# Depthwise convolution of a ConvNeXt block: filter matrices by 16 channels in three buffers, x read image by image

## The chip, the cores and the metric

The kernel runs on one core of one Trainium2 chip. The metric is the device time of one execution in microseconds; lower is better. All data are float32.

## The reference, cut to what matters

The input x is 32 images of 384 channels of 28 x 28 pixels. Layer 0 is a ConvNeXt block, layer 1 a channel gate:

```python
y = conv_general_dilated(x, dw_w, padding=[(3, 3), (3, 3)], feature_group_count=384)  # 7x7, one filter a channel
y = layernorm over channels (y + dw_b) * ln_g + ln_b
y = gelu(y @ w1 + b1)                       # 384 -> 1536
y = grn_g * (y * nx) + grn_b + y            # nx from the norm of y over the pixels
x = x + y @ w2 + b2                         # 1536 -> 384
logits = (means, maxima and minima of x over pixels, through small matrices)
x = sigmoid(logits + x)
```

The change lies in the first line, the depthwise convolution.

## The kernel before

**Two stretches.** First the depthwise convolution of all 32 images, whose result goes to HBM (`yd`, `yl`). Then, image by image, the feed-forward part: normalise, the up-projection (`up`, L901), GELU and its response norm, the down-projection (`down`, L1023), the gate. Both projections are written as a fast matrix product with fewer multiplications. Its sums of weights are made during the convolution by GpSimd (`form_w`, L585 and L587) and stored to HBM (`u1d`, `u2d`).

**The convolution as matmuls.** A 28 x 28 image is cut into blocks of 7 rows and half the width (14 columns, with the border 18). For one channel, such a block is a vector of KP = 126 numbers (18 columns by 7 rows), and the 7 x 7 filter is a banded matrix of 126 x 126 entries and more. The kernel doesn't build it entry by entry: `sequences` (L400) writes each channel's filter once as a row of FL = 268 numbers to HBM (`fs`), and `load_t` (L416) reads this row 126 times, each time shifted, into the 126 partitions of a tile `tmat`. It takes three transfers: 112 partitions of inner columns and two of 7 partitions for the edge columns, whose filters are cut. One `load_t` covers TC = 8 channels; 8 x 268 numbers are 8,576 bytes in a partition. There are NK = 48 such groups, and four `tmat` buffers.

**The x side.** `load_x` (L459) brings 16 channels of NB = 8 images into 128 partitions, one channel of one image (784 numbers, 3,136 bytes) in each, in an order of channel first and image second. There are eight buffers (seven in `room`, and `xi_last`). `pad_x` (L482) copies it with borders into `xpad`, TensorE turns it (`turn_x`, L516) into PSUM, and VectorE writes it to `xt` (L530, and L532 for the rows at the image's end). A block of XC = 16 channels (`k`) takes four such loads for the 32 images, and 24 blocks take 96.

**The order.** It is written out by hand: the loop over s (L736) takes 8 channels a turn. `conv` (L642, matmuls at L653) works on two channels at a time, four times a turn; ScalarE and VectorE move its results to `yc` (L669, L661); between these `spread` (L696) pads and turns x of the next block of 16. `load_t(s + 3)` is issued at the start of turn s. Every second turn `store` (L677) writes 16 channels to HBM. All transfers of the convolution but the filters' rows go through SP's queue in the program's order, and SP waits for a transfer's buffer before it issues the next one.

Of the kernel before, what the change touches and what calls it, by code (L numbers as in the profile page):

```python
# [8 lines left out]
F32 = mybir.dt.float32  # L9
# [4 lines left out]
P = 128  # L14
C = 384
# [4 lines left out]
NT = HW * HW  # L20
# [14 lines left out]
KP = RW * KW  # L35
NV = HW // RW
NJ = 2 * NV
NI = NV + 1
XC = 16
TC = 8  # L40
YC = 16
NB = P // XC
# [8 lines left out]
FL = 2 * PR * RW + 2  # L51
# [150 lines left out]
def convnext_gate_kernel(  # L202
# [13 lines left out]
    nc = tc.nc  # L216
    B = x.shape[0]
# [7 lines left out]
    fs = [dram.tile([3, P + 1, FL], F32, name=f"fs_{cb}") for cb in range(CB)]  # L225
# [131 lines left out]
    with ExitStack() as one:  # L357
        tp = one.enter_context(tc.tile_pool(name="tp", bufs=1))
# [33 lines left out]
        grp_a = scratch([CB, R])  # L392


        NT2 = 4
        tmat = [tp.tile([P, TC, FL], F32, name=f"tmat_{i}") for i in range(NT2)]
        nc.vector.memset(tab[:, 0], 0.0)
        nc.gpsimd.memset(tab[:, 1:], 0.0)

# [13 lines left out]
        nc.vector.memset(zrow, 0.0)  # L413
        NK = C // TC

        def load_t(s, parts=1):  # L416
            base = fs[s * TC // P]
            n = TC // parts
            for i in range(parts):
                t = tmat[s % NT2][:, i * n : (i + 1) * n, :].rearrange("k c m -> k (c m)")  # L420
                start = base.offset + (s * TC % P + i * n) * FL
                for v, e0, ne in ((0, 1, KW - 2), (1, 0, 1), (2, KW - 1, 1)):
                    nc.sync.dma_start(
                        t[e0 * RW : (e0 + ne) * RW],
                        bass.AP(
                            tensor=base.tensor,
                            offset=start + v * (P + 1) * FL + e0,
                            ap=[[1, ne], [PR, RW], [1, n * FL]],
                        ),
                    )  # L430
# [3 lines left out]
        NPAD = 3  # L434
        NWARM = 9
        xpad = [tp.tile([P, 2, NV, KW, RW], F32, name=f"xpad_{i}") for i in range(NPAD)]
# [15 lines left out]
        NX = C // XC  # L452
# [6 lines left out]
        def load_x(i):  # L459

            k, g = divmod(i, NG)
            n = i % NXI
            t = xis[i] = xi_last if n == NXI - 1 else room[:, n * NT : (n + 1) * NT]
            base = x[g * NB, k * XC : k * XC + 1, :]
            nc.sync.dma_start(
                t,
                bass.AP(
                    tensor=base.tensor,
                    offset=base.offset,
                    ap=[[NT, XC], [C * NT, NB], [1, NT]],  # L470
                ),
            )

# [34 lines left out]
        def turn_x(i, h, xt, eng=nc.vector):  # L508

            g = i % NG  # L510
            xv = xt[:KP].rearrange("p c (j b) -> p j c b", b=B)[:, h * NI : (h + 1) * NI]
            xv = xv[:, :, :, g * NB : (g + 1) * NB]
            pt = psx.tile([P, 4, P], F32, tag="pt", name=f"pt_{i}_{h}")
            for j in range(NV):
                keep(
                    nc.tensor.transpose(  # L516
                        pt[:KP, j, :],
                        xpad[i % NPAD][:, h, j].rearrange("p e r -> p (e r)"),
                        ident,
                    )  # L520
                )
            src = pt[:KP].rearrange("p j (c q) -> p j c q", q=NB)
            copies = [(xv[:, 1:NV], src[:, : NV - 1], None)]
            for v, j in enumerate((NV, 0)):
                copies.append((xv[:, j], src[:, NV - 1], ends[:KP, v : v + 1]))
            for d, p, mask in copies:
                if eng is nc.scalar:
                    eng.activation(d, p, AF.Identity, scale=1.0 if mask is None else mask)
                elif mask is None:
                    eng.tensor_copy(d, p)  # L530
                else:
                    eng.tensor_scalar(d, p, mask, None, ALU.mult)  # L532
# [59 lines left out]
        def pad_next(i):  # L592
            nonlocal loaded
            if i < GT:
                pad_x(i)
                while loaded < min(GT, i + 1 + NXI):
                    load_x(loaded)
                    loaded += 1

        for i in range(NG):  # L600
            load_x(i)
        xt = new_xt(0)
        for i in range(NG):
            pad_x(i)
            if i == 0:
                load_t(0, 2)
                nc.sync.dma_start(dwb, cvec[0:1, :].broadcast_to([P, C]))
            if i == NG - 2:
                for cb in range(CB):
                    if cb:  # L610
                        keep(sequences(cb))
                    keep(nc.scalar.dma_start(fs[cb][:, P:, :].rearrange("v o m -> o v m"), zrow))
            if i == NG - 2:

                nc.gpsimd.tensor_copy(tmat[1][:, 0, :1], xpad[i % NPAD][:, 0, 0, 1, :1])
                load_t(1)
            load_x(NG + i)
            for h in range(2):
                turn_x(i, h, xt, (nc.vector, nc.scalar)[h])
# [19 lines left out]
        SK = XC // TC  # L639
        PAIRS = TC // 2  # L640

        def conv(s, c2, yc, xt):  # L642

            t = tmat[s % NT2]
            pc = psc.tile([P, 2, NJ * B], F32, tag="pc", name=f"pc_{s}_{c2}")
            for ci in range(2):
                c = 2 * c2 + ci
                for h, up_, down_ in ((0, UP_L, DOWN_L), (1, UP_R, DOWN_R)):
                    po = pc[:, ci, h * NV * B : (h + 1) * NV * B]
                    xc = xt[:KP, s % SK * TC + c, h * NI * B : (h + 1) * NI * B]  # L650
                    for n, (m0, j) in enumerate(((up_, 1), (down_, 0))):
                        keep(
                            nc.tensor.matmul(  # L653
                                po, t[:KP, c, m0 : m0 + P], xc[:, j * B : (j + NV) * B],
                                start=(n == 0), stop=(n == 1),
                            )
                        )
            cc = s * TC + 2 * c2
            cy = cc % YC
            if c2 % 2:  # L660
                nc.vector.tensor_tensor(  # L661
                    yc[:, :, :, cy : cy + 2].rearrange("p b j c -> p c j b"),
                    pc.rearrange("p c (j b) -> p c j b", j=NJ),
                    dwb[:, cc : cc + 2].unsqueeze(2).unsqueeze(3).to_broadcast([P, 2, NJ, B]),
                    ALU.add,
                )
            else:
                for ci in range(2):
                    nc.scalar.activation(  # L669
                        yc[:, :, :, cy + ci].rearrange("p b j -> p j b"),  # L670
                        pc[:, ci, :].rearrange("p (j b) -> p j b", j=NJ),
                        AF.Identity,
                        bias=dwb[:, cc + ci : cc + ci + 1],
                        scale=1.0,
                    )
# [20 lines left out]
        def spread(k, q, xn):  # L696
            for n in plan[q]:
                g, h = divmod(n, 2)
                i = k * NG + g
                if h == 0:  # L700
                    pad_next(i + 1)
                turn_x(i, h, xn)
# [32 lines left out]

        for s in range(NK):  # L736
            k, si = divmod(s, SK)
            if s + 3 < NK:
                if s == 0:
                    for i in range(2, 4):  # L740
                        nc.gpsimd.tensor_copy(tmat[i][:, 0, :1], xpad[i % NPAD][:, 0, 0, 1, :1])
                        if i == 2:
                            load_t(i)
                load_t(s + 3)
            if s in later:

                dst, src = later[s]
# [11 lines left out]
            for c2 in range(PAIRS):  # L759
                conv(s, c2, yc, xt)  # L760
                if k + 1 < NX:
                    spread(k + 1, si * PAIRS + c2, xn)
# [35 lines left out]
            i = s - U1  # L798
# [454 lines left out]
```

## Time and profile before

| what | before |
|---|---|
| median of 3 runs | 3149.55 us (3147.44 to 3153.77) |
| the profiled execution, its time | 3145.94 us |
| its span, first to last instruction | 3144.2 us |
| TensorE busy (PE) | 3048.0 us, 97% |
| VectorE (DVE), ScalarE (ACT), GpSimd (POOL) busy | 2059.3, 2146.3, 2265.0 us |
| first matmul of the up-projection | 538.5 us from the start |
| bytes moved | 653.84 MB, 208 GB/s on average |
| convolution matmuls, L653 | 3072, busy 385.9 us |

The profile is of one execution. A slice is a fortieth of the span, and its digit the busy share in tenths. Instructions stand in groups by line, engine and tile; "<-" names what ended the idle time before them. A DMA issue is an instruction of SP (SPq); the bytes then go as packets over the core's 16 DMA engines, and the DMA share is the mean busy share of the 16. A busy TensorE is not TensorE at its peak, since matmuls overlap.

### The profile page before, as it was taken

What the parts mean: (1) busy time and instruction counts of PE and PEld (TensorE: products, weight loads), DVE (VectorE), ACT (ScalarE), POOL (GpSimd) and SP (SyncE); (2) the same over time, 40 slices, a digit from 0 to 9 for tenths busy, and PEclk for the clock granted to TensorE, in tenths of its full rate; (3) what the DMA queues carried; (4) which work ended last, traced back from release to release, by engine and by line L of the source; (5) the groups of instructions that cost most, each with busy time, mean ns of one, the idle gap of its engine ahead of it and who ended that gap; (6) DMA issues with size and microseconds to landing.
All of it is one profiled execution on the core that took longest, in us unless ns stands there. A gap on an engine that the chain in (4) does not pass through costs nothing.

```text
span 3144.2 us, 48626 instructions
## 1 busy us (share of the span) xinstructions
PE 3048.0 (97%) x15913; PEld 2490.0 (79%) x15913; DVE 2059.3 (65%) x5833; ACT 2146.3 (68%) x3458; POOL 2265.0 (72%) x1776
## 2 busy tenths in 40 slices
PE   7798989999999999999999999999999999999997
PEld 7798988577777777777777777777777777777777
DVE  5565566766666666666666666666666666666665
ACT  5565664857777777777777777777777777777771
POOL 1231533398888788888888888888888888888887
PEclk9999999999999999999999999999999999999999
DMA  9999999455665666566656566555555566656545
GB/s 257 277 321 308 316 307 322 149 167 190 196 197 191 194 197 195 191 196 197 190 190 189 187 196 192 187 188 187 189 190 189 189 192 193 191 190 192 192 153 187
DMA packets 317388, 653.84 MB, mean 208 GB/s; under 512 B 30227, under 2 KB 143668, under 8 KB 308144
## 3 DMA queue, kind: packets, MB, share of 16 engines
q1 hardware_dynamic: 303520, 612.15, 62.2%
q10 hardware_dynamic: 13618, 38.58, 3.1%
q8 instruction: 130, 2.13, 0.3%
q14 instruction: 120, 0.98, 0.1%
HBM read 549.13 MB, written 101.51 MB: 207 GB/s over the span
## 4 chain that ended last, share of the span: by engine, by line
PE 76%; DMA 16%; POOL 3%; DVE 3%; issue 1%; ACT 0%; SPq 0%; ACTq 0%; POOLq 0%; DVEq 0%
PE ph_C L901 12%; PE ph_B L901 12%; PE ph_A L901 12%; DMA tmat<-fs 8%; PE pz_A L1023 7%; PE pz_C L1023 7%; PE pz_D L1023 7%; PE pz_F L1023 6%; DMA yi<-yd 3%; PE py L859 2%; PE pc L653 2%; PE pz_E L1023 2%; DMA room<-in_x 2%; PE pz_H L1023 2%; DMA yd<-yc 2%; POOL d_room L984 2%
## 5 line engine op out<-in xcount | busy, mean ns | idle before, releaser
L984 POOL TENSOR_TENSOR d_room<-y 128x588 f32<-128x588 f32 x257 | 368.4, 1439 | 348.3 <-PE pz_B L1023 199.7
L315 ACT ACTIVATE y<-y,fv,gsc 128x784 f32<-128x784 f32 x376 | 362.9, 1031 | 364.9 <-DVE gsc L937 364.9
L871 ACT ACTIVATE y<-y,fv 128x784 f32<-128x784 f32 x384 | 349.9, 945 | 195.9 <-DVE y L916 173.9
L901 PE MATMUL ph_C<-room,ws 128*128 128x392 f32 x1240 | 460.4, 493 | 2.1 <-DVE y L910 1.8
L901 PE MATMUL ph_B<-room,ws 128*128 128x392 f32 x1240 | 459.4, 493 | 2.3 <-issue 1.8
L901 PE MATMUL ph_A<-room,ws 128*128 128x392 f32 x1240 | 459.2, 492 | 2.0 <-POOL room L353 2.0
L984 POOL TENSOR_TENSOR d_room<-d_room,y 128x588 f32<-128x588 f32 x309 | 442.6, 1437 | 14.6
L653 PE MATMUL pc<-xt,tmat 126*128 126x128 f32 x3072 | 385.9, 283 | 55.1 <-DMA tmat<-fs 53.3
L653 PEld LDWEIGHTS pc<-xt,tmat 126*128 126x128 f32 x3072 | 370.2, 198 | 61.2 <-issue 49.3
L901 PEld LDWEIGHTS ph_C<-room,ws 128*128 128x128 f32 x1240 | 234.3, 190 | 178.1 <-issue 9.5
L901 PEld LDWEIGHTS ph_A<-room,ws 128*128 128x128 f32 x1240 | 235.3, 190 | 175.3 <-POOL room L353 2.6
L901 PEld LDWEIGHTS ph_B<-room,ws 128*128 128x128 f32 x1240 | 234.4, 190 | 166.9 <-DVE te L914 2.2
L984 POOL TENSOR_TENSOR d_room<-y,d_room 128x588 f32<-128x588 f32 x220 | 315.9, 1436 | 45.9 <-PE pz_A L1023 18.2
L877 ACT ACTIVATE junk<-y 128x784 f32<-128x784 f32 x384 | 328.4, 855 | 6.9
L353 POOL TENSOR_TENSOR room<-room 128x392 f32<-128x392 f32 x300 | 300.4, 1018 | 11.8
L984 POOL TENSOR_TENSOR y<-y 128x588 f32<-128x588 f32 x188 | 269.7, 1435 | 7.3
L478 ACT ACTIVATE xpad<-room 128x357 f32<-128x357 f32 (+2 forms) x320 | 188.1, 631 | 115.6 <-DMA room<-in_x 58.1
L585 POOL TENSOR_SCALAR u<-ws 128x384 f32<-128x384 f32 (+1 forms) x53 | 66.5, 1260 | 243.6 <-DMA u2d<-u 129.1
L1045 DVE TENSOR_REDUCE stq<-x 128x1 f32<-128x196 f32 x768 | 224.9, 348 | 2.5
L912 DVE TENSOR_TENSOR y<-y,ph_B 128x392 f32<-128x392 f32 x256 | 134.5, 554 | 140.1 <-ACT y L871 123.5
L910 DVE TENSOR_TENSOR y<-y,ph_C 128x392 f32<-128x392 f32 x384 | 211.3, 556 | 22.3
L1023 PE MATMUL pz_A<-d_room,u 128*128 128x196 f32 x1056 | 203.8, 329 | 0.0
(226 smaller groups left out, 6193.5 us busy)
## 6 DMA issues: line engine op xcount, KB each, us to landing
u<-u2d SPq DMA_DIRECT2D x487, 384.0 KB
ws<-u1d SPq DMA_DIRECT2D x384, 320.0 KB
ws<-u2d SPq DMA_DIRECT2D x121, 384.0 KB
yd<-yc SPq DMA_DIRECT2D x22, 2048.0 KB
tmat<-fs SPq DMA_DIRECT2D x47, 938.0 KB
yi<-yd SPq DMA_DIRECT2D x31, 1408.0 KB
x<-in_x SPq DMA_DIRECT2D x32, 1176.0 KB
out<-x ACTq DMA_DIRECT2D x31, 1176.0 KB
```

The lines of the kernel that those rows point to most:

```text
L315: eng.activation(out, in_, AF.Identity, bias=add, scale=mul)
L353: tc.keep_in_program_order(eng.tensor_tensor(d, o[in0], o[in1], op))
L478: eng.activation(dst, src, AF.Identity)
L653: nc.tensor.matmul(po, t[:KP, c, m0 : m0 + P], xc[:, j * B : (j + NV) * B], start=(n == 0), stop=(n == 1),)
L871: nc.scalar.activation(y, y, AF.Gelu, bias=b1_t[:, f : f + 1], scale=1.0)
L877: nc.scalar.activation(junk, ys[b][:, f, :], AF.Square, accum_out=ssqs[b][:, f : f + 1])
L901: nc.tensor.matmul(banks[t, bk][:, :NH], wts[t][:, i % UG, :], o[opnd], start=(first == 1), stop=True, skip_group_check=True,)
L910: nc.vector.tensor_tensor(d, d, p, ALU.add)
L912: nc.vector.tensor_tensor(d, d, p, ALU.subtract)
L984: nc.gpsimd.tensor_tensor(d[0], o[a][0], o[c][0], ALU.add if sign == "+" else ALU.subtract)
L1023: nc.tensor.matmul(pz[:, :NQ4], wt[:, i % UD, t, :], o[opnd][0][:, t, :], start=(first and t == 0), stop=(t == KD - 1), skip_group_check=True,
L1045: nc.vector.tensor_reduce(stq[:, v, m, h : h + 1], xh, AX.X, op2)
```

## The change

`load_t` now takes a block of 16 channels, the block that `xt` has, so a tile `tmat` is twice as wide and a partition gets 17,152 bytes in one run. There are three buffers in place of four, and the load is issued in every second turn, two blocks ahead. `conv` picks its 8 channels out of the 16. Independently of this, `load_x` now puts image first and channel second in the 128 partitions: 16 neighbouring channels of one image follow each other, as they do in HBM. `turn_x` reads its PSUM result in the order that belongs to it, so `xt` is the same as before.

```diff
-        NT2 = 4
-        tmat = [tp.tile([P, TC, FL], F32, name=f"tmat_{i}") for i in range(NT2)]
+        NT2 = 3
+        tmat = [tp.tile([P, XC, FL], F32, name=f"tmat_{i}") for i in range(NT2)]
...
-        def load_t(s, parts=1):
-            base = fs[s * TC // P]
-            n = TC // parts
+        def load_t(k, parts=1):
+            base = fs[k * XC // P]
+            n = XC // parts
             for i in range(parts):
-                t = tmat[s % NT2][:, i * n : (i + 1) * n, :].rearrange("k c m -> k (c m)")
-                start = base.offset + (s * TC % P + i * n) * FL
+                t = tmat[k % NT2][:, i * n : (i + 1) * n, :].rearrange("k c m -> k (c m)")
+                start = base.offset + (k * XC % P + i * n) * FL
...
-                    ap=[[NT, XC], [C * NT, NB], [1, NT]],
+                    ap=[[C * NT, NB], [NT, XC], [1, NT]],
...
-            src = pt[:KP].rearrange("p j (c q) -> p j c q", q=NB)
+            src = pt[:KP].rearrange("p j (q c) -> p j c q", q=NB)
...
-            t = tmat[s % NT2]
+            t = tmat[s // SK % NT2]
...
-                                po, t[:KP, c, m0 : m0 + P], xc[:, j * B : (j + NV) * B],
+                                po, t[:KP, s % SK * TC + c, m0 : m0 + P], xc[:, j * B : (j + NV) * B],
...
-            if s + 3 < NK:
-                if s == 0:
-                    for i in range(2, 4):
-                        nc.gpsimd.tensor_copy(tmat[i][:, 0, :1], xpad[i % NPAD][:, 0, 0, 1, :1])
-                        if i == 2:
-                            load_t(i)
-                load_t(s + 3)
+            if si == 0 and k + 2 < NX:
+                if k == 0:
+                    nc.gpsimd.tensor_copy(tmat[2][:, 0, :1], xpad[2 % NPAD][:, 0, 0, 1, :1])
+                load_t(k + 2)
```

## The prediction

> **What bounds the kernel now.** I read the page's slices first, to see which stretch differs from the rest.
>
> ```profile
> PE   7798989999999999999999999999999999999997
> DMA  9999999455665666566656566555555566656545
> ```
>
> One slice is 78.6 us. In the first seven the DMA engines are full and TensorE is not; from the eighth on it is the other way round. The change touches only code of the first stretch, the depthwise convolution. Next the busy time by stretch; the columns are length, PE, PEld, DVE, ACT, POOL, granted clock, DMA share, GB/s. The first feed-forward matmul (L901) starts at 538.5 us, so I cut at 537.
>
> ```profile
> 0.00:100.00 100.00, 74.39 (x587) 71.89 (x588) 51.42 (x127) 57.10 (x108) 15.99 (x40) 0.95 0.94 253
> 100.00:200.00 100.00, 88.45 (x753) 87.13 (x752) 57.58 (x135) 61.96 (x113) 24.00 (x20) 0.97 1.01 307
> 300.00:400.00 100.00, 93.32 (x797) 91.92 (x796) 60.91 (x141) 67.26 (x120) 51.75 (x50) 0.97 0.99 318
> 537.00:3144.00 2607.00, 2581.62 (x12008) 2032.23 (x12008) 1753.30 (x5097) 1823.26 (x2877) 2090.55 (x1590) 1.00 0.59 189
> ```
>
> A DMA share of 0.94 to 1.01, with no compute engine over 0.94: the convolution ends when its transfers end. The chain of waits, cut to its first 537 us, and the waits themselves say which transfers:
>
> ```profile
> by line: DMA tmat<-fs 47.1%; PE pc L653 13.4%; DMA room<-in_x 11.4%; DMA yd<-yc 9.9%; DMA u2d<-u 3.5%; PE pt L516 2.4%; DMA xi_last<-in_x 2.0%; DMA yi<-yd 1.8%; issue 1.5%; ACT xpad L478 1.0%; DMA fs<-ws 0.9%; SPq L465 0.8%; SPq L423 0.7%;
> ...
> ACT xpad L478 <- DMA room<-in_x: 58.1, 21, 8.7
> PE pc L653 <- DMA tmat<-fs: 53.3, 27, 7.8
> ```
>
> All of them stand in one SP queue, so the name of the last one says little: what counts is how long the 16 engines need for all of them. The DMA view of the same 537 us gives the transfers:
>
> ```profile
> q1 hardware_dynamic: 51656, 159.70, 96.5%
> ...
> tmat<-fs SPq DMA_DIRECT2D x47, 938.0 KB
> room<-in_x SPq DMA_DIRECT2D x84, 392.0 KB
> ...
> tmat<-fs SPq DMA_DIRECT2D x94, 58.6 KB
> xi_last<-in_x SPq DMA_DIRECT2D x12, 392.0 KB
> ```
>
> The trace also keeps every packet with its size and time, and one packet is one row. To 540 us, on SP's queue: 12,288 rows of x (3,136 B), 195 ns on average, the fastest tenth 124 ns; 5,922 filter rows (8,576 B), 463 ns, the fastest tenth 324; 2,944 stored rows (16,384 B), 629 ns. About 16 packets are in flight at every moment, one for each engine.
>
> [...]SP issues 1,422 transfers in the whole run: [...]1,323 have k = 16, the 98 edge transfers of the filters (7 partitions) k = 7, the one of 24 rows k = 12, together 21,168 + 686 + 12 = 21,866 semaphore writes. The records hold 28,394 four-byte packets on that queue, and 6,528 of them are the elements of `fv` and `cv` (128 x 36 and 128 x 15), which leaves 21,866.
> [...]from 40 to 48 us all 16 engines load x, [...]and they reach 257 GB/s; later 16 engines load the 2,560-byte rows of `ws`, and most rows take 102 ns, which is 25 GB/s an engine.
>
> **The change part by part.**
> (a) x read image by image. The source's slowest dimension was 16 channels and becomes 8 images; the destination has 128 partitions. [...]The row count, row size and bytes stay, but 96 transfers of 128 rows now lie on engines 0 to 7 alone: 1,536 rows each in place of 768.
> What an engine has to do now, to 540 us: x 12,288 x 195 / 16 = 150 us. Filters: the 8,576-byte rows 5,922 x 463 / 16 = 171, the first tile's half rows 4, together 175 as a mean; of 126 rows 112 go to all 16 engines, 175 x 112/126 = 156 us, and the 14 edge rows to engines 0 to 6, 175 x 14/126 x 16/7 = 44. Stores 116, rows of 512 B 21, of 1,536 B 31, of 6,144 B 9, all small ones 8. Engines 0 to 6: 535 us of 540. Engines 7 to 15: 491. So engines 0 to 6 already set the end, and the change adds to just these.
> The price of an x row among eight engines isn't in the trace. Lower bound 124 ns, the row alone: 1,536 x 124 = 190 us, +40. Today's mean 195: 300 us, +150. Upper bound 248[...]: 381 us, +231. For: with engines 8 to 15 off x there is less to collide with.[...] I take 170 ns, about two thirds of the way from 124 to 195: 261 us, **+111 us**. Nothing covers it: [...]TensorE already waits for them. A covered cost would need engines 0 to 6 to have slack, and they have 5 us.
> (b) Filters by 16 channels. Twice the row (17,152 B), half the rows, the same bytes and the same k (16 and 7). Two 4,288-byte rows cost 2 x 166 ns at best, one of 8,576 B 324: 8 ns saved for each pair joined. Engines 0 to 6 have 48 x (7 + 2) = 432 such rows and get 216: 216 x 8 ns, so -2 us. SP's issues at L423 fall from 147 to 75, 72 x 0.4 us = 29 us less on SP's sequencer; SP isn't the bound, so 0. The first convolution still needs 0.94 MB of filters, but the x loads queued next stand behind 0.94 MB more, at 250 GB/s 4 us; these bytes are missing later, so I take 0 (-5 to +5).
> (c) Three buffers of 16. A load of block k+2 waits for the matmuls of block k-1, which ended just before; the old one of s+3 waited for s-1, likewise. What stands behind it in SP's queue (x loads, a store of `yc`) waits no longer than now. Look-ahead grows from 3 half blocks to 2 blocks; with the engines full, looking ahead buys nothing: 0. SBUF grows by 3 x 17,152 - 4 x 8,576 = 17,152 B a partition, and the pools after the convolution wait for its last reader as before: 0, at most 2.
> (d) `turn_x` on VectorE reads PSUM with a step of 16 elements (L530, L532: 103.3 + 113.2 us busy). No such read is in the trace; the nearest, L313 reading PSUM backwards with steps, takes 0.69 us for 392 elements where L530 takes 0.55 for 384, a quarter more. A quarter of 217 is 54 us more of VectorE, which is busy 57 of 100; even doubled (+217) it would stay under the stage's length. Below nothing isn't possible for a step added: 0, hidden by the idle half of VectorE; if DMA's cover went, VectorE at 306 + 54 us would still be behind TensorE.
> Sum: 111 - 2 = +109 us on the profiled execution, 3145.9 us (span 3144.2), so 3255. That execution lies 3.6 us under the median of the runs, 3149.55, so I say **3258 us**. The 2,607 us after the convolution are bound by TensorE (2,581.6 busy) and stay.
>
> **The rivals.**
> 1. *Eight engines at the full rate.* With half the engines on x no row meets another: 124 ns, +40, less the 2 us: 3188. The fastest tenth of rows speaks for it[...].
> 2. [...]200 to 248 ns: +157 to +231, 3305 to 3378. For: x alone on 16 engines gave 257 GB/s, not 400.[...]
> 3. *The faster side: the transfers stay on 16 engines*[...], and reading one image at a time ends the collisions: a row falls from 195 to 124, 768 x 71 = 55 us saved, 3093. It decides from the point where x has 11 engines at that rate (12,288 x 124 ns / 150 us = 10.2). The exact packet count speaks against it. On eight engines it can't get there: 150 us in 1,536 rows is 98 ns, or 32 GB/s an engine, and no row of x went under 124.
> 4. *Nothing moves:* another resource than engines 0 to 6 bounds the stage, and eight idle engines only look bad: within 6 us. Against: 535 of 540 us.
>
> **How the numbers follow.** Main case (around 170 ns, +70 to +150) 0.60; rival 1 0.16, rival 2 0.15, rival 3 0.05, rival 4 0.04. For 8 in 10 the range runs from just under the full-rate case to inside rival 2: 3185 to 3325. Slower 0.91, same 0.04, faster 0.05; 0.2% is about what a measurement of this kernel can tell from no change.
>
> **What would show it.** In the changed kernel: the first L901 matmul near 650 us in place of 538; x's transfers with 8 semaphore writes each, 768 packets fewer; in the convolution's slices a DMA share near 0.75 to 0.8 and about 245 GB/s in place of 301, with TensorE near 0.7; more waiting for `room<-in_x` at L478; VectorE's L530 at 0.55 to 0.7 us; and the stretch after it 2,607 us. It is wrong if the stage's DMA share stays near 1, if the waits move to VectorE, or if x's transfers still post 16 writes.

## The result and the profile after

The changed kernel takes 3239.9 us (median of 4 runs, 3237.99 to 3245.05), the kernel before in the same session 3151.66 us. The ratio is 1.0284, with a 95% interval of 1.0265 to 1.0302: 88 us slower. The forecast was 3258 us, in a range of 3185 to 3325.

First the slices of the changed kernel, a slice being 81 us here:

```profile
PE   6787788899999999999999999999999999999998
DMA  7788778744556666555565656665666555656545
```

The convolution now takes the first eight slices, and its DMA digits are 7 and 8 where they were 9. The transfers take longer although the DMA engines are less busy on average. The busy time by stretch of the changed kernel says the same; the columns are length, PE, PEld, DVE, ACT, POOL, granted clock, DMA share, GB/s:

```profile
100.00:200.00 100.00, 74.03 (x576) 72.19 (x576) 45.01 (x108) 51.49 (x92) 19.38 (x19) 0.88 0.78 246
300.00:400.00 100.00, 72.00 (x598) 70.21 (x597) 45.21 (x106) 52.13 (x93) 20.68 (x20) 0.91 0.79 268
640.00:3239.00 2599.00, 2576.90 (x11991) 2029.64 (x11989) 1748.50 (x5086) 1820.39 (x2871) 2090.60 (x1590) 1.00 0.59 189
```

These are two stretches of 100 us and all that follows the convolution. The two have a DMA share of 0.78 and 0.79 and TensorE at 0.72 to 0.74. The granted clock is lower too: over the whole stage 0.90 (to 633 us) where it was 0.96 (to 537 us), and TensorE is busy for 491 us where it was 466. No run held the clock. It was 0.94 in e1 and e4 below, 0.91 in e2 and 0.83 in e3, so it went down as TensorE's waits grew; that it is a consequence and not a cause is argued from this. The timeline of TensorE dates the end of the stage, by the first matmul of the up-projection (start, length, instruction):

```profile
633.83 2.41 PE L898 MATMUL ph_B<-room,ws 128*128 128x392 f32 x6 [1.77 <-issue]
```

It was at 538.5 us before, so the convolution is 95 us longer in the two profiled executions (3241.6 and 3145.9 us, 96 apart), and the feed-forward part has the length it had. The chain of waits of the changed kernel, cut to its first 628 us, and what TensorE itself waits for there (us in total, times, longest):

```profile
by line: DMA yd<-yc 38.6%; PE pc L653 16.1%; DMA room<-in_x 15.7%; DMA tmat<-fs 11.4%; ACT xpad L478 3.4%; ACT yc L669 2.8%; DMA u2d<-u 2.3%; PE pt L516 2.0%; DMA fs<-ws 1.7%; DVE yc L661 1.3%; SPq L465 1.1%; issue 0.7%; POOL u L585 0.4%; S
...
PE pc L653 <- ACT yc L669: 54.4, 13, 7.0
PE pc L653 <- DVE yc L661: 36.9, 7, 9.0
PE pt L516 <- ACT xpad L478: 20.2, 9, 5.6
PE pc L653 <- DMA tmat<-fs: 13.6, 7, 4.1
```

This is a new picture. Before, TensorE waited for the filters (53.3 us); now it waits for ScalarE and VectorE to empty PSUM into `yc` (54.4 and 36.9, together 91 us), and the chain runs through the stores of `yc`. Whether that is a cause or only the place where a general lack of transfer time shows is the question of half the experiments.

The packet records answer what the forecast asked of them. x's transfers have 8 semaphore writes: 20,378 four-byte packets of semaphores on SP's queue, 1,488 fewer than before, which are 768 for x (96 x 8) and 720 for the 24 filter loads that are gone, with 16 + 7 + 7 each. The k of the forecast is this number of a transfer's writes; that x's would be 8 was assumed there. A row of x takes 154 ns on average (195 before). A filter row of 17,152 B takes 894 ns (two of 8,576 took 926).

The packets' times count from the start of the trace, and the first instruction, from which all other times here count, comes 11 us later. The prediction didn't allow for this: its "540 us" end at 529 us of the profile, and its "40 to 48 us" of x alone are 29 to 37. Its sum of 535 us for engines 0 to 6 thus stands against 529 us, and there were not even 5 us of slack. From here on, packets are counted on the profile's clock too.

Up to the landing of the last filter row, engines 0 to 6 of the changed kernel have, in us: x 12,288 x 154 / 8 = 237, filters 170 x 112/126 + 170 x 14/126 x 16/7 = 194, stores 109, the rest 63, in all 602 or 603, and that row lands at 606 us. The same sum gives 530 of 519 us before, and 623 of 601 us in e2 below: it is right to some 20 us, and within that there is no slack. Engines 8 to 15 have much: for some 160 us of the first 560 exactly eight packets are in flight. Which engine a packet ran on isn't recorded: engines 0 to 7 stand here for those that carry x, 0 to 6 for those that carry the edge rows. That the seven are among the eight was assumed in the forecast, and the changed kernel's packets agree: in the 89 us up to 606 us in which rows of x and one to seven filter rows are in flight and nothing else is, they are eight together for 75 us, most often 7 filter rows and 1 of x (22.8 us) or 1 and 7 (19.7 us).

### The profile page after: what moved, and what is told of

The parts are those of the page before. It is cut to its first block, busy times and chain, and to the rows that moved or that the text cites. A ratio compares the mean times of both kernels' runs of the same rounds, so it can differ in the third digit from the quotient of the medians.

```text
span 3239.9 us, 48430 instructions
## 1 busy us (share of the span) xinstructions
PE 3074.4 (95%) x15913; PEld 2512.9 (78%) x15913; DVE 2058.0 (64%) x5833; ACT 2149.6 (66%) x3458; POOL 2264.7 (70%) x1775
## 4 chain that ended last, share of the span: by engine, by line
PE 76%; DMA 16%; POOL 3%; DVE 2%; ACT 1%; issue 1%; SPq 0%; ACTq 0%; POOLq 0%; DVEq 0%
PE ph_C L898 12%; PE ph_A L898 12%; PE ph_B L898 12%; DMA yd<-yc 7%; PE pz_A L1020 7%; PE pz_C L1020 7%; PE pz_D L1020 6%; PE pz_F L1020 6%; PE pc L653 3%; DMA room<-in_x 3%; PE py L856 2%; DMA tmat<-fs 2%; DMA yi<-yd 2%; PE pz_E L1020 2%; PE pz_H L1020 2%; PE pz_I L1020 1%
## 5 line engine op out<-in xcount | busy, mean ns | idle before, releaser
L653 PE MATMUL pc<-xt,tmat 126*128 126x128 f32 x3072 | 406.1, 292 | 105.7 <-ACT yc L669 54.4
L653 PEld LDWEIGHTS pc<-xt,tmat 126*128 126x128 f32 x3072 | 390.5, 208 | 112.1 <-ACT yc L669 57.4
L898 PE MATMUL ph_B<-room,ws 128*128 128x392 f32 x1240 | 459.4, 493 | 2.8 <-issue 1.8
L898 PE MATMUL ph_C<-room,ws 128*128 128x392 f32 x1240 | 460.3, 493 | 1.8 <-DVE y L907 1.5
L898 PE MATMUL ph_A<-room,ws 128*128 128x392 f32 x1240 | 459.2, 492 | 0.3 <-POOL room L353 0.3
L898 PEld LDWEIGHTS ph_C<-room,ws 128*128 128x128 f32 x1240 | 234.3, 190 | 177.7 <-issue 8.9
L898 PEld LDWEIGHTS ph_A<-room,ws 128*128 128x128 f32 x1240 | 235.3, 190 | 173.6 <-DVE y L909 2.4
L898 PEld LDWEIGHTS ph_B<-room,ws 128*128 128x128 f32 x1240 | 234.4, 190 | 167.4 <-DVE te L911 2.7
L353 POOL TENSOR_TENSOR room<-room 128x392 f32<-128x392 f32 x300 | 300.5, 1018 | 11.8
L669 ACT ACTIVATE yc<-pc,dwb 128x256 f32<-128x256 f32 x192 | 107.9, 687 | 200.3 <-PE pc L653 140.8
L478 ACT ACTIVATE xpad<-room 128x357 f32<-128x357 f32 (+1 forms) x320 | 183.1, 629 | 81.4 <-DMA room<-in_x 78.3
```

The costliest lines, as they stand in the source:

```text
L353: tc.keep_in_program_order(eng.tensor_tensor(d, o[in0], o[in1], op))
L478: eng.activation(dst, src, AF.Identity)
L653: nc.tensor.matmul(po, t[:KP, s % SK * TC + c, m0 : m0 + P], xc[:, j * B : (j + NV) * B], start=(n == 0), stop=(n == 1),)
L898: nc.tensor.matmul(banks[t, bk][:, :NH], wts[t][:, i % UG, :], o[opnd], start=(first == 1), stop=True, skip_group_check=True,)
```

## The experiments

All ratios are to the kernel before, run on the same chip in the same call, with 95% intervals. "Stage" is the start of the first up-projection matmul in the profiled execution, and the row times are the mean durations of its packets. Each stage comes from one execution, and that of the kernel before (3145.9 us) lies 6 to 10 us under the medians of its sessions (3151.7 to 3155.8), so a difference of less than some 10 us between two stages says nothing.

| run | ratio | stage, us | x row, ns | filter row, ns |
|---|---|---|---|---|
| before | 1 | 538.5 | 195 | 463 |
| changed kernel | 1.0284 [1.0265, 1.0302] | 633.8 | 154 | 894 (double) |
| e1_filters_only | 1.0095 [1.0071, 1.0119] | 573.0 | 205 | 1018 (double) |
| e2_x_only | 1.0262 [1.0244, 1.0281] | 620.8 | 164 | 449 |
| e3_4_engines | 3412.3 us, one run | 801.6 | 136 | 921 (double) |
| e4_16_engines | 1.0114 [1.0094, 1.0133] | 576.6 | 204 | 1026 (double) |
| e5_halves_apart | 1.0056 [1.0037, 1.0074] | 555.0 | 201 | 468 |
| e6_halves_together | 1.0064 [1.0047, 1.0080] | 561.4 | 198 | 508 |
| e7_no_edges | 0.9910 [0.9890, 0.9930] | 518.4 | 200 | 493 |
| e9_x_by_ports | 0.9986 [0.9977, 0.9995] | 536.0 | 183 | 475 |
| e10_apart_order | 1.0018 [1.0006, 1.0031] | 553.2 | 200 | 474 |
| e11_wide_order | 1.0102 [1.0067, 1.0137] | 577.9 | 203 | 1032 (double) |
| e12_after_order | 1.0268 [1.0233, 1.0303] | 632.8 | 152 | 902 (double) |
| e13_ports_order | 0.9986 [0.9975, 0.9997] | 540.5 | 181 | 468 |

### One part alone

```diff
 # e1_filters_only, against the changed kernel
-                    ap=[[C * NT, NB], [NT, XC], [1, NT]],
+                    ap=[[NT, XC], [C * NT, NB], [1, NT]],
...
-            src = pt[:KP].rearrange("p j (q c) -> p j c q", q=NB)
+            src = pt[:KP].rearrange("p j (c q) -> p j c q", q=NB)
```

> Edit: the wide filter tiles and three buffers stay, load_x and turn_x get the old order (channel first). Theory (the loss is x on 8 engines instead of 16, engines 0 to 6 set the end): x has 16 semaphore writes a transfer again, the first L898 matmul is at 530 to 545 us, the time 3143 to 3157 us, no different from before. Rival A (the wide tiles cost: 1.88 MB in one burst ahead of x in SP's queue, or fewer buffers): part of the 88 us stays, 3170 us or more.

Measured: 1.0095, 3186 us, as rival A said. x is back on 16 engines, yet 30 us of loss stay: the wide filter tiles cost by themselves.

The opposite half, `e2_x_only`, makes the two opposite edits in the kernel before.

> Edit: the kernel before, with only load_x and turn_x in the new order. Theory: the whole loss is here, 3225 to 3250 us, x rows at about 154 ns on average. Rival A (wide tiles): 3150 to 3190 us.

Measured: 1.0262, 3236.7 us, x rows 164 ns. So nearly the whole loss is in the order of x, where rival A fails, and the two halves don't add up: 30 and 81 to 88. The changed kernel is only 7 us over e2, and their intervals overlap: with x on eight engines the tiles cost little or nothing more. That their 30 us are hidden there behind a wait that is there anyway is argued. In this kernel TensorE waits where it waited before the change, only twice as long:

```profile
PE pc L653 <- DMA tmat<-fs: 109.8, 31, 9.8
```

Rows of x were faster here than before (164 against 195 ns) and still a wait of 53 us grew to 110: there are twice as many on the engines that count.

### The number of engines or the order of the addresses

```diff
 # e4_16_engines, against the changed kernel
-            base = x[g * NB, k * XC : k * XC + 1, :]
+            c0 = k * XC + g // 2 * (XC // 2)
+            base = x[g % 2 * 2 * NB, c0 : c0 + 1, :]
...
-                    ap=[[C * NT, NB], [NT, XC], [1, NT]],
+                    ap=[[C * NT, 2 * NB], [NT, XC // 2], [1, NT]],
 # e3_4_engines, against the changed kernel
-            base = x[g * NB, k * XC : k * XC + 1, :]
+            c0 = k // 2 * 2 * XC
+            base = x[(k % 2 * NG + g) * NB // 2, c0 : c0 + 1, :]
...
-                    ap=[[C * NT, NB], [NT, XC], [1, NT]],
+                    ap=[[C * NT, NB // 2], [NT, 2 * XC], [1, NT]],
```

> Edit: the changed kernel, but a transfer of x is 16 images by 8 neighbouring channels in place of 8 images by 16, so x is still read image by image, in runs of 25 KB, and the source's slowest dimension is 16; turn_x writes the matching part of xt. Theory (number of engines): 16 semaphore writes a transfer, x rows back at 180 to 200 ns, 3140 to 3165 us. Rival B (the order of the addresses, images 1.2 MB apart in lock step, costs the time in HBM): 3220 us or more.

> Edit: the changed kernel with transfers of 4 images by 32 channels: every row of x is still read once, but the rows land in other places than turn_x expects, so the output has the pixels of the wrong images and channels. Theory: 4 semaphore writes a transfer, 3,072 rows on each of engines 0 to 3. The other work of these engines is 618 - 237 = 381 us by the packet records of the changed kernel; 3,072 x 124 to 154 ns is 381 to 473 us; stage 760 to 860 us, time 3365 to 3465 us. Rival B (HBM order): runs of 100 KB are longer still, so about the 3240 us of the changed kernel or less.

Measured: e4 1.0114, which is e1's ratio within the intervals (1.0094 to 1.0133 and 1.0071 to 1.0119), with e1's row times. It misses its stated 3140 to 3165 us by just the tiles' cost, which the expectation didn't know of. The comparison it was made for is with e1: reading image by image costs nothing that these runs can tell as long as 16 engines read. With 4 engines the time is 3412 us, the stage 801.6 us, inside what the engines' load gave (760 to 860; by the sum above the other work is 365 us and not 381, and the range holds). Rows then take 136 ns, near the 124 of the fastest tenth before: 12,288 x 136 / 4 = 418 us of x on each of four engines. Sixteen, eight and four engines (e4, the changed kernel, e3), all image by image, in runs of 25, 50 and 100 KB: 576.6, 633.8, 801.6. Four-byte packets give 16, 8 and 4 semaphore writes a transfer of x. The rows get faster from step to step (204, 154, 136 ns) and the stage longer. The number of engines is the cause.

### Is it the busiest engines, or all bytes?

```diff
 # e7_no_edges, against the kernel before; the tiles are set to zero once at the start
-                for v, e0, ne in ((0, 1, KW - 2), (1, 0, 1), (2, KW - 1, 1)):
+                for v, e0, ne in ((0, 1, KW - 2),):
```

> Edit: the kernel before without the two edge transfers of each filter tile (14 of 126 rows; the edge columns' filters are zero in place). These rows lie on engines 0 to 6 alone, 2 each a tile, 44 us of an engine's time. Theory (engines 0 to 6 set the end): 38 to 46 us less, 3105 to 3118 us. Rival F (all bytes together set it): 5.8 MB at 301 GB/s are 19 us, about 3132 to 3138 us.

Measured: 0.9910, 29 us less (22 to 35 by the interval): more than the bytes' share, less than the engines', and outside both stated ranges. Both numbers were computed with fixed row times, and these moved: x rows 200 in place of 195 ns, filter rows 493 in place of 463. Up to the last filter row, each of the 16 engines now has 153 for x, 166 for filters, 111 for stores and 65 for the rest, together 495 of 498 us. So the load of an engine still accounts for the time, but this run doesn't decide between the busiest engines and all bytes: the stage of its profiled execution is 20 us shorter (518.4 for 538.5), close to the bytes' 19. The decision lies in e2, e3 and e4, where the bytes stayed and the number of engines changed.

### Why the wide tiles cost 30 us

TensorE's waits for `yc` led to ScalarE's queue. Its timeline, first of the kernel before, then of the changed one (start, length, instruction, idle before):

```profile
383.65 1.18 ACT L669 ACTIVATE yc<-pc,dwb 128x256 f32<-128x256 f32 x2
384.62 0.85 ACT L478 ACTIVATE xpad<-room 128x357 f32<-128x357 f32 x1
386.36 1.61 ACT L478 ACTIVATE xpad<-room 128x357 f32<-128x357 f32 x3 [0.89 <-PE pt L516]
388.26 1.18 ACT L669 ACTIVATE yc<-pc,dwb 128x256 f32<-128x256 f32 x2 [0.29 <-PE pc L653]
```

```profile
385.39 2.35 ACT L478 ACTIVATE xpad<-room 128x357 f32<-128x357 f32 x4 [0.86 <-DMA room<-in_x]
388.22 2.39 ACT L478 ACTIVATE xpad<-room 128x357 f32<-128x357 f32 x4 [0.48 <-DMA room<-in_x]
390.51 2.37 ACT L478 ACTIVATE xpad<-xi_last 128x357 f32<-128x357 f32 x4
393.85 2.34 ACT L478 ACTIVATE xpad<-room 128x357 f32<-128x357 f32 x4 [0.96 <-DMA room<-in_x]
398.68 2.12 ACT L669 ACTIVATE yc<-pc,dwb 128x256 f32<-128x256 f32 x4 [2.49 <-DMA yd<-yc]
```

With wide tiles the layer that orders the instructions puts 8 results and then 16 pads in a row, block after block; before, results stood between the pads. Nothing in the diff says so. In the lines above, four results of ScalarE stand behind 16 pads, three groups of which wait for x, and then wait 2.49 us more for a store that frees `yc`. VectorE's results (L661) are bunched as well: in e5 two in a row stand behind the copies of six pieces of x into `xt`, where before each stood alone. Four kernels take this apart: filters in halves again, in their own turns or together, and with ScalarE held in the written order.

```diff
 # e5_halves_apart, against e1_filters_only (in load_t: for i in range(parts) if half is None else (half,))
-            if si == 0 and k + 2 < NX:
-                if k == 0:
+            if k + 2 < NX:
+                if s == 0:
...
-                load_t(k + 2)
+                load_t(k + 2, 2, si)
 # e6_halves_together, against e1_filters_only
-                load_t(k + 2)
+                load_t(k + 2, 2)
 # e10, e11, e12, e13: against e5, e1, the changed kernel and e9
-                eng.activation(dst, src, AF.Identity)
+                keep(eng.activation(dst, src, AF.Identity))
...
-                    nc.scalar.activation(
+                    keep(nc.scalar.activation(
```

> Edit: e1_filters_only (old x order, three wide tiles), but each tile is loaded in two halves of 8 channels, the first in the even turn and the second in the odd turn, so SP's queue has the small loads between x and stores as the kernel before. Theory C (the 1.0% of e1 comes from one long stretch of filter rows on all engines at once, in which [...]no store lies beside them): 3148 to 3163 us. Rival D (three buffers, or the time at which a load may start): stays at 3178 to 3190 us.

> Edit: e1_filters_only, but a tile is loaded in two halves that are issued one right after the other: rows of 8,576 B again, the same stretch of 1.88 MB. Theory C: nothing gained over e1, 3175 to 3195 us. Rival E (rows of 17,152 B are slower in themselves[...]): back to 3148 to 3163 us.

> Edit: e5_halves_apart with ScalarE's pads (L478) and results (L669) held in the written order. In all kernels with wide tiles ScalarE's queue has 8 results and then 16 pads in a row for each block, where the kernel before has results between the pads; a pad that waits for x then holds up the results behind it, and TensorE waits for the PSUM they would free. Theory H (this order is what e5's 0.6% comes from): TensorE's waits for yc fall from 57 us to under 15, 3146 to 3160 us. Rival (the order is harmless, three buffers cost): stays at 3165 to 3175 us.

> Edit: e1_filters_only with ScalarE held in the written order. Theory H with C (order and burst each cost a part): the order's part goes, the burst's part of e1 over e5 (12 to 15 us) stays, 3160 to 3175 us. If the order is everything: 3146 to 3160. If it is nothing: 3178 to 3190.

Measured: e5 1.0056 and e6 1.0064 can't be told apart, so in the time it makes no difference where the halves stand in the queue, and theory C falls in this form; both lie between their stated ranges. Against e1 (1.0095) e5 gains about 12 us and e6 about 10, though the ends of the intervals still overlap. The row times do show theory C's burst: with the halves together a pair of rows takes 2 x 508 = 1016 ns, as much as e1's wide row (1018), and with the halves apart 2 x 468 = 936. So, with x on 16 engines, slow filter rows go with the long stretch and not with the width of a row, and rival E falls.

In e5 the row times are back, and the last filter row lands at 519 us as before; what is left of its loss lies in TensorE's waits. With the written order, e5 becomes e10 at 1.0018: the intervals (1.0037 to 1.0074 and 1.0006 to 1.0031) don't meet, so the order is worth about 12 us there by the medians. The profiled executions show only 2 of them (555.0 and 553.2), as that of e5 was the fastest of its four. e10's median of 3162 us is 2 over the stated range in a session whose kernel before took 3155.8. TensorE's waits, in e5 and in e10 (whose lines are numbered 2 higher, L516 as L518):

```profile
PE pc L653 <- DVE yc L661: 56.8, 20, 4.2
PE pt L516 <- ACT xpad L478: 10.8, 4, 5.3
```

```profile
PE pt L518 <- ACT xpad L480: 62.1, 38, 6.6
```

The wait for `yc`, which was for VectorE's results, is gone, as theory H said, and VectorE's results stand singly again. What takes its place is a longer wait for the pads, so the gain is less than the wait that went. The pads now stand behind ScalarE's results, and these wait for stores that free `yc` (85 us in e10), while the pads themselves wait only 15 us for x.

In e11, though, the order brings nothing (1.0102 against 1.0095, 3190.9 us: the third case of the expectation). With the whole tile in one transfer something else counts. SP's own waits show a candidate, in e1 and then in the kernel before:

```profile
SPq L681 <- DMA tmat<-fs: 77.6, 15, 8.7
SPq L465 <- DMA tmat<-fs: 41.1, 8, 7.7
```

```profile
SPq L681 <- DMA room<-in_x: 12.7, 16, 1.5
```

L681 issues the store of `yc`. In the traces SP's transfers use eight semaphores in turn (101 to 108; up to the first up-projection matmul 335 of 341 transfers before and 264 of 268 in the changed kernel follow in this order), and SP waits, before a transfer, for the same semaphore's last one, eight places ahead in its queue (331 of 341 and 259 of 268 show this wait). In e1 that is a filter transfer, and a store waits 5 us for it; before, it was a load of x, 0.8 us.

That these late stores make the loss is not shown, and the packet records speak against it. They divide the time up to the last filter row into stretches without and with stores of `yc` in flight:

| run | without, us | GB/s | with, us | GB/s |
|---|---|---|---|---|
| before | 302 | 255 | 218 | 366 |
| e1_filters_only | 335 | 227 | 210 | 368 |
| e6_halves_together | 349 | 237 | 187 | 379 |

The time grows by 26 us from before to e1. But the bytes moved without stores are the same (77 and 76 MB): it is not that more reads stood alone, the reads that stood alone were slower. And e6 has less time beside stores than e1 and is the faster of the two. By rows: e1's wide filter row takes 92 ns more than two rows before, and 216 of them on each of engines 0 to 6 make 20 us; 768 rows of x at 10 ns more make 7. Why filter rows in one long stretch are slower stays open.

The rest of e1's loss is plain. From the last filter row's landing to the first up-projection matmul it is 19 us before and in e2 (519.2 to 538.5; 601.5 to 620.8), 28 in e1 and in the changed kernel (545.3 to 573.0; 606.0 to 633.8): sixteen channels of matmuls are left to do, where it was eight.

> Edit: the changed kernel with ScalarE held in the written order. Theory (engines 0 to 6 set the end, 618 us of 634): TensorE's waits for yc (91 us) turn into waits for the filters, and little is gained: 3222 to 3238 us. Rival I (the 88 us are the order's, x on 8 engines only adds to the pads' waits): 3150 to 3200 us.

Measured: 1.0268, inside the changed kernel's interval, and 3241.5 us, above the stated 3222 to 3238: nothing is gained at all. TensorE's 91 us of waits for `yc` went, but not into waits for the filters, as the theory had it. In their place, up to 628 us, stand a wait of TensorE and behind it one of ScalarE:

```profile
PE pt L518 <- ACT xpad L480: 121.3, 47, 10.9
ACT yc L671 <- DMA yd<-yc: 167.2, 21, 16.1
```

TensorE waits for pads, and the pads stand behind results of ScalarE that wait for stores to free `yc`; for x itself the pads wait 16 us. So in the changed kernel the order of ScalarE's queue, conspicuous as it is in the waits, decides only where TensorE stands still. e2 says the same from the other side: its ScalarE has the order of the kernel before, and it loses 81 us.

### 128 rows at one step, and a kernel that beats both

```diff
 # e9_x_by_ports, against the kernel before; dw_w, dw_b, ln_g, ln_b and w1 are loaded in the same order of channels
-            base = x[g * NB, k * XC : k * XC + 1, :]
+            base = x[0, i : i + 1, :]
...
-                    ap=[[NT, XC], [C * NT, NB], [1, NT]],
+                    ap=[[C // 4 * NT, P], [1, NT]],
...
-            xv = xv[:, :, :, g * NB : (g + 1) * NB]
+            xv = xv[:, :, 4 * g : 4 * g + 4, :]
...
-            src = pt[:KP].rearrange("p j (c q) -> p j c q", q=NB)
+            src = pt[:KP].rearrange("p j (b m) -> p j m b", m=4)
```

> Edit: the kernel before with another assignment of channels: a transfer of x is 32 images by the 4 channels i, i+96, i+192, i+288, which in HBM is one run of 128 rows at one step, so source and destination both have a slowest dimension of 128 (dw_w, the bias, the norm's gain and bias and w1's rows are loaded in the matching order; nothing is left out). Theory[...]: x rows fall from 195 to 124 to 140 ns on 16 engines, 42 to 55 us off engines 0 to 6, 3100 to 3120 us. Rival G (a limit in HBM on x[...]): rows stay at 180 to 200 ns, 3140 to 3160 us.

> Edit: e9_x_by_ports with ScalarE held in the written order, to see whether there is more to be had than e9. Theory (the transfers bound this kernel too, its order was good before): 3138 to 3152 us, no different from e9. If the order helps here also: 3120 to 3138 us.

Measured: e9 0.9986 (0.9977 to 0.9995), 4 us in place of the 42 to 55; e13, with the written order, the same. The rate is there where x is alone: from 29 to 32 us after the first instruction all 16 engines load x at 409 GB/s, where the kernel before had 254 from 29 to 37 us. Why the rows are faster in this shape isn't shown. And x is seldom alone. Beside filter rows in flight its rows take 199 ns (196 before); the mean falls only from 195 to 183 ns, and the filter rows go from 463 to 475. Twelve ns of 768 rows are 9 us, 12 ns of 432 filter rows on engines 0 to 6 give 5 back: 4 us. That this is just what was measured is partly luck, since the sum is right to some 20 us. e9 and e13 are the only kernels here that leave nothing out and are faster than the kernel before, by 0.14%.

## Why the prediction was right

Right in direction, in the mechanism of the main term and in size (+109 stated, +88 measured). The nearness of the two sizes is in part luck: by e2, (a) was about 30 us too high, (b) and (c) about 9 too low.

- **Bound.** Engines 0 to 6 set the end. Confirmed by 16, 8 and 4 engines (e4, changed, e3). e7 agrees with it but doesn't decide, and row times give way when the load changes.
- **(a), +111 us.** Right in cause, too large. The row was taken at 170 ns and took 154 in the changed kernel: 237 us against 150, +87, close to the 88 lost. In e2, with this part alone, it took 164, which gives +103, and the run lost 81 us. Why the rows were nearer to the lower bound isn't shown. The reason given, that engines 8 to 15 are off x, fits e2 (148 ns with at most nine packets in flight, 176 with more), but not the changed kernel (160 and 150).
- **(b), -2 us, and (c), 0.** Wrong, by about 30 us where they are alone (e1). In (b) the joined row was taken to save 8 ns; in e1 it cost 92 more, 20 us in all. In (c) what stands behind the filter load in SP's queue "waits no longer than now"; a store waits 5 us in place of 0.8, though this isn't shown to cost time. And two steps are missing: the queues of ScalarE and VectorE are put in another order, and 16 channels in place of 8 are left to do behind the last landing, 9 us that were foreseeable. In the changed kernel a joined row took 32 ns less than two before, and the tiles' cost all but disappears.
- **(d), 0.** Right: L530 takes 551 ns, 549 before.
- **Rivals.** The first (rows at 124, 3188) and the second (rows at 200 to 248, 3305 and more) are on both sides of the result; 248 was an estimate, twice the fastest tenth. Rows of x did go under 124 ns before, but only 29 of 12,288, and none under 121. The third is excluded by the 8 semaphore writes, the fourth by the result itself and by e3.
- **Signs.** The DMA share of 0.75 to 0.8 came, and TensorE was at 0.72 to 0.85 after the first 100 us, somewhat over the stated 0.7. Throughput was 246 to 269 GB/s from 100 to 600 us, the L898 matmul came at 634 in place of 650, and the wait for `room<-in_x` at L478 grew from 58 to 78 us. One sign of being wrong came in part: waits moved to VectorE (36.9 us) and ScalarE. e12 shows that they decide nothing.

## What to carry to other kernels

Before an access pattern is turned round, work out on how many engines its transfers will run: with 16, 8 and 4 in the slowest dimension of its source, a transfer of x posted 16, 8 and 4 semaphore writes here (e4, the changed kernel, e3). A load that reads longer runs in HBM on half of the DMA engines lost 81 us (e2), and the longer runs gained nothing. Work out what each engine has to move, not the mean over 16, and multiply by a row time that may change with the load. When a transfer becomes wider, compare the order of every engine's queue in the two built programs, and ask what is issued behind the transfer and what work is left behind the last one. Put all times on one clock before setting a sum against them. And a long wait in a profile is a cause only if a run without it is faster (e12).

## What had not been expected of the hardware

- Rows of x on 16 engines with 128 rows at one step on both sides: 409 GB/s while x was alone (e9); the same rows as 16 x 8: 254 GB/s. Among other transfers the advantage all but goes (183 and 195 ns on average).
- With x on 16 engines, filter rows in one long stretch were slower than in two (e6, e5: 508 and 468 ns for the same 8,576 B).
- VectorE reading PSUM with a step of 16 elements, 126 x 384: 551 ns, without 549.
- Mean row times of the same transfers moved with what the other engines did (x rows 152 to 205 ns with 8 or 16 engines), so sums with fixed row times went wrong: 44 us were expected off engines 0 to 6 in e7 and 29 gained, by the medians.
